# Products of zeros on TensorE between the steps of a selective-scan kernel

## The chip, the cores and the metric

The kernel runs on one core of a Trainium2 chip. The metric is the device time of one execution in microseconds (us), the median of several runs. The profile is of one further execution, taken by the hardware profiler.

## What is computed

The reference takes an image batch of 4 x 64 x 64 positions with 96 channels through four layers. Two are selective scans (state-space layers), two are attention without a softmax followed by a small quantized network. Nearly all the time goes into the two scan layers. Cut to what matters, one of them does this for each of 4 orders k in which the 4,096 positions are read:

```python
xc = silu(conv3x3_depthwise(in_proj(group_norm(x))) + conv_b)
dts, Bs, Cs = split(x_proj_k @ xs_k)            # 6 + 16 + 16 rows
delta = softplus(dt_w_k @ dts + dt_b_k)         # 192 channels
h_t = exp(delta_t * A) * h_(t-1) + (delta_t * u_t) * B_t     # 192 channels x 16 states
y_t = sum over the 16 states of h_t * C_t
y = sum over k of (y + Ds * xs), put back into image order
x = x + out_proj(layer_norm(y) * silu(z))
```

## The kernel before

**Tiles.** The scans are cut into 3,072 tiles. A tile is one state pair for 64 of the 192 channels over 1,024 positions: 128 partitions hold 64 channels of two images or states, the free dimension holds 1,024 positions. The list `tiles` (L1030) runs over 64 blocks `at`, each a phase (layer and pair of images), an order k and a quarter t of the positions; in a block over 2 groups g of 8 state numbers n, over 3 thirds j of the channels, and innermost over the 8 n of the group. So a block has 48 tiles, and a group of 8 tiles sums into one accumulator `py` in PSUM (tag psY, one buffer of two banks).

**What one tile needs.** For tile i, with `f` a buffer in SBUF (6 of them) and `psB` one in PSUM (2 of them):

- `begin` (L656): ScalarE writes the decays exp(delta*A) into f (`decays`, L679). For the five n in POOL_N (1, 4, 7, 10, 13) GpSimd writes the inputs du*B into f instead (L662), and ScalarE writes the decays into psB.
- `row` (L667): for the other eleven n, TensorE spreads the rows of B over the partitions with two bf16 products with the selection matrix `sel` into psB (L672). It has to wait until the scan of tile i-2 has left that psB.
- `product` (L683): VectorE multiplies psB by delta*u (L686).
- `scan` (L688): VectorE runs the recurrence over 1,024 positions into f (L694). ScalarE keeps the last column as the next state (L700).
- `weigh` (L702): GpSimd multiplies by C (L705).
- `gather` (L738): for every second tile, TensorE adds two tiles into `py` with four fp32 products with `fold`, a 128 x 64 matrix of two identities (L745). This frees both f.
- At the end of a group of 8, `flush` (L750) has ScalarE copy py away (L757 or L761), and `resume` (L725) has ScalarE write into the same py what the next group's sum begins with (L731, L733 or L736).

**The order.** The engines' orders of work are written out by hand (`manual_schedule`) in the loop at L1065. In step i the calls come in this order: `begin(i+2)`, `flush(i-3)` and `resume(i-2)` at a group's end, `gather(i-2)` where that n is odd, `row(i+2)`, `scan(i)`, the decays of a POOL_N tile i+2, `product(i+1)`, `weigh(i)`. Each engine works through its own instructions in that order. After these calls come side jobs: the next block's preparation (`prepare`, L511: projections L552, cuts L568 and L572, steps L579), and pieces of a generator (`behind`, L1015) that runs the next convolution (`conv_pieces`, L214) or the layer norm and output projection of an earlier phase (`tail_pieces`, L320). In the trace a full-precision (fp32) product appears as two records, a bf16 product as one.

After the last scan step come the two attention layers and their networks, under a planner (`run`, L776) that the change doesn't touch.

Of the kernel before, what the change touches and what calls it, by code (L numbers as in the profile page):

```python
# [8 lines left out]
F32 = mybir.dt.float32  # L9
# [18 lines left out]
NG = 2  # L28
GN = N // NG
MANUAL = {mybir.EngineType.PE, mybir.EngineType.DVE, mybir.EngineType.Activation, mybir.EngineType.Pool}  # L30
POOL_N = (1, 4, 7, 10, 13)


@with_exitstack
def kernel(ctx: ExitStack, tc: tile.TileContext, ins, out, layers=(0, 1, 2, 3)):
# [72 lines left out]

    minus = wp.tile([96, 2 * N], BF16, tag="minus", name="minus")
    nc.vector.tensor_scalar_mul(minus, m32[0:96], -1.0)  # L110


    def per_channel(name, cols, src, tag):
# [100 lines left out]
    def conv_pieces(w, xin, xc, zg, done):  # L214

        norms = []

        def part_of(n):
            xb = wide([C, T], "xb")
            nc.sync.dma_start(xb, xin[n // NT][:, n % NT * T : (n % NT + 1) * T])  # L220
            return xb

        xbs = [part_of(n) for n in range(3)]
        for _ in range(4):
            yield free()
        for i in range(2):
            stats = small([C, NT, 6], "gst")
            for t in range(NT):
                if t:
                    yield free()  # L230
                nc.vector.bn_stats(stats[:, t, :], xbs.pop(0))
                if i * NT + t + 3 < 2 * NT:
                    xbs.append(part_of(i * NT + t + 3))
            mv = small([C, 2], "gmv")
            nc.vector.bn_aggr(mv, stats)
            yield free(2)
            pm = psM([C, 1])
            nc.tensor.matmul(pm, gmat, mv[:, 0:1], start=True, stop=True)
            yield held(1)
            mean = small([C, 1], "gmean")  # L240
            nc.vector.tensor_copy(mean, pm)
            dev = small([C, 1], "gdev")
            nc.vector.tensor_sub(dev, mv[:, 0:1], mean)
            nc.vector.tensor_mul(dev, dev, dev)
            nc.vector.tensor_add(dev, dev, mv[:, 1:2])
            yield free(2)
            pv = psM([C, 1])
            nc.tensor.matmul(pv, gmat, dev, start=True, stop=True)
            yield held(1)
            t = small([C, 1], "grs")  # L250
            nc.vector.tensor_scalar_add(t, pv, 1e-5)
            scale = small([C, 1], f"gscale{i}")
            nc.gpsimd.tensor_tensor(scale, t, mhalf[0:C, 0:1], ALU.pow)
            yield free()
            shift = small([C, 1], f"gshift{i}")
            nc.vector.scalar_tensor_tensor(shift, mean, -1.0, scale, ALU.mult, ALU.mult)
            norms.append((scale, shift))
        if "join" in w:
            w.pop("join")()
        rows = T // HW  # L260

        def load(t):
            pads = []
            for i in range(2):
                r0, r1 = t * rows - 1, (t + 1) * rows + 1
                lo, hi = max(r0, 0), min(r1, HW)
                pad = wide([C, rows + 2, HW + 2], "pad")
                nc.vector.memset(pad[:, :, 0:1], 0.0)
                nc.vector.memset(pad[:, :, HW + 1 : HW + 2], 0.0)
                if lo > r0:  # L270
                    nc.vector.memset(pad[:, 0, 1 : HW + 1], 0.0)
                if hi < r1:
                    nc.vector.memset(pad[:, rows + 1, 1 : HW + 1], 0.0)
                inner = pad[:, lo - r0 : hi - r0, 1 : HW + 1]
                nc.sync.dma_start(inner, xin[i][:, lo * HW : hi * HW].rearrange("p (r c) -> p r c", c=HW))
                pads.append((pad, inner))
            return pads

        outs = []
        done.append(now[0])  # L280
        coming = load(0)
        yield free()
        yield free()
        for t in range(NT):
            pads, coming = coming, None
            for i in range(2):
                nc.scalar.activation(pads[i][1], pads[i][1], AF.Identity, bias=norms[i][1], scale=norms[i][0])  # L287
            yield free(6)
            for j in range(J):
                if outs:  # L290
                    outs.pop()()
                if j == J - 1 and t + 1 < NT:
                    coming = load(t + 1)
                px = psM([128, T])
                for tap in range(9):
                    for i in range(2):
                        nc.tensor.matmul(  # L297
                            px[64 * i : 64 * i + 64], w["wf"][:, tap, 64 * j : 64 * j + 64],
                            pads[i][0][:, tap // 3 : tap // 3 + rows, tap % 3 : tap % 3 + HW],
                            start=(tap == 0), stop=(tap == 8),  # L300
                        )
                    yield held(10 - tap, tap < 8)
                xo = thin([128, T], "xo")
                nc.scalar.activation(xo, px, AF.Silu, bias=w["cb"][:, j, :])
                pz = psM([128, T])
                for i in range(2):
                    nc.tensor.matmul(
                        pz[64 * i : 64 * i + 64], w["wz"][:, 64 * j : 64 * j + 64],
                        pads[i][0][:, 1 : 1 + rows, 1 : 1 + HW], start=True, stop=True,
                    )  # L310
                yield held(1)
                zo = thin([128, T], "zo")
                nc.scalar.activation(zo, pz, AF.Silu)
                nc.sync.dma_start(xc[:, j, t * T : (t + 1) * T], xo)
                outs.append(lambda j=j, t=t, zo=zo: nc.sync.dma_start(zg[:, j, t * T : (t + 1) * T], zo))
                yield free(6 if j < J - 1 else 0)
            outs.pop()()
            done[0] += 1

    def tail_pieces(w, units, y, zg, xin, xout, tokens):  # L320
# [11 lines left out]
        for t in units:  # L332
# [28 lines left out]
            for q in range(2):  # L361
                pt = psM([128, 2, D])
                for j in range(J):
                    nc.tensor.matmul(
                        pt[:, :, 64 * j : 64 * j + 64], yu[:, j, q * 128 : (q + 1) * 128], ident, start=True, stop=True
                    )
                if q:
# [58 lines left out]
            if tokens:  # L426
                xo = thin([128, 2, 2, C], "xn")
                pos = []
                for i in range(2):
                    half = slice(64 * i, 64 * i + 64)  # L430
                    pos.append(psM([128, 2, 128]))
                    for q in range(2):
                        tok = slice(q * 128, (q + 1) * 128)
                        o = pos[i][:, q, 0:C]
                        nc.tensor.matmul(o, xr[:, i, tok], ident[0:C, 0:C], start=True, stop=False)
                        for j in range(J):
                            nc.tensor.matmul(o, zu[half, j, tok], w["ow"][half, j, :], start=False, stop=(j == J - 1))  # L437
                    yield held(2 - i)
                for i in range(2):
                    nc.scalar.copy(xo[:, i], pos[i][:, :, 0:C])  # L440
# [5 lines left out]
            else:  # L446
                xo = thin([C, 2, U], "xn")
                pos = []
                for i in range(2):
                    half = slice(64 * i, 64 * i + 64)  # L450
                    pos.append(psM([C, U]))
                    nc.tensor.matmul(pos[i], ident[0:C, 0:C], xr[:, i, :], start=True, stop=False)
                    for j in range(J):
                        nc.tensor.matmul(pos[i], w["ow"][half, j, :], zu[half, j, :], start=False, stop=(j == J - 1))
                    yield held(2 - i)
                for i in range(2):
                    nc.scalar.copy(xo[:, i, :], pos[i])
# [53 lines left out]
    def prepare(ph, k, t):  # L511
# [37 lines left out]
        def project(s, j):  # L549
            if j == 0:  # L550
                pps.append(psM([76, T]))
            nc.tensor.matmul(  # L552
                pps[s], order[0][0][:, j, :], xs[j][:, halves[s]], start=(j == 0), stop=(j == J - 1)
            )

# [13 lines left out]

        def take(s, q):  # L570
            part = slice(32 * q, 32 * q + 32)
            nc.tensor.matmul(  # L572
                pps[s][0 : 2 * N], minus[part], p["parts"][part, halves[s]], start=False, stop=True,
                skip_group_check=True,
            )

        def steps(s, j):
            pds.append(psM([128, T]))
            nc.tensor.matmul(  # L579
                pds[-1], order[0][1][64:76, j, :], rests[s][64:76], start=True, stop=True  # L580
            )

# [84 lines left out]
    def row(i):  # L667
        at, g, j, n = tiles[i]
        if n not in POOL_N:
            for s in range(2):  # L670
                ss = slice(s * T, (s + 1) * T)
                nc.tensor.matmul(  # L672
                    scanned[i][0][:, ss], sel[:, n, :], made[at]["parts"][:, ss], start=True, stop=True
                )

# [36 lines left out]
    def unlock():  # L712
        py = psY()
        for s in range(2):
            for q in range(T // 128):
                o = s * T + q * 128
                nc.tensor.matmul(py[:, o : o + 128], ident, ident, start=(q == 0), stop=True, skip_group_check=True)

    def recall(i):
        at, g, j, n = tiles[i]  # L720
# [17 lines left out]
    def gather(i):  # L738
# [3 lines left out]
        for s in range(2):  # L742
            ss = slice(s * T, (s + 1) * T)
            for e in range(2):
                nc.tensor.matmul(  # L745
                    py[64 * e : 64 * e + 64, ss], fold, two[e][:, ss],
                    start=False, stop=(n == g * GN + GN - 1), skip_group_check=True,
                )

    def flush(i):  # L750

# [284 lines left out]
    with tc.manual_schedule(engines=MANUAL):  # L1036
# [28 lines left out]
        for i in range(-9, end + 4):  # L1065
# [9 lines left out]
                resume(i - 2)  # L1075
            if 0 <= i - 2 < end and tiles[i - 2][3] % 2:
                gather(i - 2)
            if 0 <= i + 2 < end:
                row(i + 2)
            if 0 <= i < end:  # L1080
# [151 lines left out]
```

## Time and profile before

| | |
|---|---|
| median of 3 runs | 11,288.7 us (11,288.23 to 11,288.97) |
| the profiled execution's own time | 11,291.6 us |
| its span | 11,289.8 us |
| granted TensorE clock, mean | 0.814 of full speed |
| scans, L694 | 3,072, mean 2.27 to 2.35 us by kind |
| weighings on GpSimd, L705 | 3,072 of 2.354 us |
| inputs on GpSimd, L662 | 960 of 2.359 us |
| gathers, L745 | 12,288 records of fp32 products |
| first scan | 130 us after the start |

DVE is VectorE, ACT is ScalarE, POOL is GpSimd, PE is TensorE and PEld its weight loads, which overlap its products. A busy share is over the whole span. In a row of groups the numbers after the bar are busy us and the mean ns of one instruction, and after a second bar the idle time of that engine just before them, and who ended most of it. A row of waits reads "who waited <- for whom: us in total, times, longest us". PEclk is the clock granted to TensorE, in tenths of full speed by slice; in finer windows it is either 1.00 or 0.50, and the record changes only at steps of 3.41 us.

### The profile page before, as it was taken

The page shows a single profiled execution, that of the slowest core. Times are in us where ns is not written, and L with a number is a line of the kernel's source. Part 1 is how long each engine was busy: PE and PEld are TensorE (multiplying, and loading weights), DVE is VectorE, ACT ScalarE, POOL GpSimd, SP SyncE. Part 2 cuts the span into 40 slices and gives each one's busy share as a digit, 9 for nine tenths or more (in the row PEclk, how much of TensorE's full clock was granted, in tenths as well). Part 3 has the DMA queues.
Part 4 walks back from the last instruction along what each step waited for, and adds up shares of the span by engine and source line. Part 5 has one row for each costly group of instructions (what it writes and reads, how often), then busy time and mean ns, then how long its engine had stood idle before and what let it go on. Part 6 is the DMA issues. An engine that isn't in the chain of part 4 may idle for free. (4 is left out here: it accounts for less than half of the span.)

```text
span 11289.8 us, 97780 instructions
## 1 busy us (share of the span) xinstructions
PE 8418.7 (75%) x27696; PEld 2658.3 (24%) x27696; DVE 9945.0 (88%) x6431; ACT 7094.3 (63%) x11231; POOL 10199.5 (90%) x5102
## 2 busy tenths in 40 slices
PE   7877778766777777877677776788777776677776
PEld 2212122111222221222122221222122222112365
DVE  3898899999999899988999999899999999999845
ACT  3657666555666665677566665676566665556676
POOL 3889899999999898989999999999999999999846
PEclk8878888877888787888878888888887877887876
DMA  5669876897678885698656656665566565556410
GB/s 131 154 141 156 137 154 155 153 132 133 150 165 147 135 163 150 139 157 146 145 146 170 155 143 149 156 166 141 149 159 158 140 157 145 141 135 155 123 39 18
DMA packets 1848972, 1605.07 MB, mean 142 GB/s; under 512 B 1412330, under 2 KB 1483692, under 8 KB 1848428
## 3 DMA queue, kind: packets, MB, share of 16 engines
q1 hardware_dynamic: 1848428, 1598.83, 65.0%
q8 instruction: 218, 3.57, 0.1%
q14 instruction: 326, 2.67, 0.1%
HBM read 1009.16 MB, written 186.65 MB: 106 GB/s over the span
## 5 line engine op out<-in xcount | busy, mean ns | idle before, releaser
L705 POOL TENSOR_TENSOR f<-f,crep 128x1024 f32<-128x1024 f32 x3072 | 7159.4, 2354 | 482.4 <-DVE f L694 354.0
L745 PE MATMUL psY<-f,fold 128*64 128x512 f32 x12288 | 4261.9, 771 | 675.3 <-issue 292.9
L694 DVE TENSOR_TENSOR_SCAN f<-f,state,psB 128x1024 f32<-128x1024 f32 x1584 | 3718.3, 2347 | 226.3 <-ACT f L679 65.7
L672 PE MATMUL psB<-spB,sel 96*128 96x512 bf16 x4224 | 1484.2, 439 | 1927.9 <-DVE f L694 1878.9
L686 DVE TENSOR_TENSOR psB<-psB,du 128x1024 f32<-128x1024 f32 x2112 | 2558.2, 1211 | 368.2 <-PE psB L672 327.2
L679 ACT ACTIVATE f<-delta,L_a 128x1024 f32<-128x1024 f32 x2112 | 2407.4, 1145 | 667.2 <-PE psY L745 571.5
L662 POOL TENSOR_TENSOR f<-du,brep 128x1024 f32<-128x1024 f32 x960 | 2264.2, 2359 | 211.9 <-DMA crep<-bc 81.0
L694 DVE TENSOR_TENSOR_SCAN f<-psB,state,f 128x1024 f32<-128x1024 f32 x720 | 1678.5, 2331 | 168.9 <-ACT psB L679 132.5
L745 PEld LDWEIGHTS psY<-f,fold 128*64 128x64 f32 x12288 | 1079.3, 166 | 3138.4 <-issue 2189.0
L700 ACT COPY state<-f 128x1 f32<-128x1 f32 x2304 | 427.2, 186 | 1842.0 <-DVE f L694 1832.7
L679 ACT ACTIVATE psB<-delta,L_a 128x1024 f32<-128x1024 f32 x960 | 1069.2, 1114 | 563.9 <-DVE f L694 536.6
L694 DVE TENSOR_TENSOR_SCAN f<-f,psB 128x1024 f32<-128x1024 f32 x528 | 1207.9, 2288 | 56.5 <-ACT f L679 6.3
L672 PEld LDWEIGHTS <-sel 96*128 96x128 bf16 x4224 | 284.1, 101 | 3768.8 <-DVE f L694 2436.4
L297 PE MATMUL psM<-pad,wf 96*64 96x512 f32 x3456 | 912.9, 645 | 11.6 <-ACT pad L287 8.4
L694 DVE TENSOR_TENSOR_SCAN f<-psB,f 128x1024 f32<-128x1024 f32 x240 | 545.6, 2273 | 98.5 <-ACT psB L679 57.3
L595 POOL TENSOR_TENSOR xs<-delta,xs 128x1024 f32<-128x1024 f32 x192 | 452.5, 2357 | 90.4 <-ACT delta L592 90.4
L579 PE MATMUL psM<-proj,dtw 12*128 12x512 f32 x768 | 526.4, 783 | 0.2 <-ACT spB L568 0.2
L552 PE MATMUL psM<-xs,xp 128*76 128x512 f32 x768 | 429.2, 671 | 12.7 <-DMA xp<-in_L_xp 5.1
L761 ACT COPY ynew<-psY 128x1024 f32<-128x1024 f32 (+2 forms) x312 | 242.6, 819 | 195.3 <-PE psY L745 195.0
L297 PEld LDWEIGHTS psM<-pad,wf 96*64 96x64 f32 x3456 | 234.2, 144 | 511.3 <-issue 463.2
L586 ACT ACTIVATE delta<-psM,L_dtb 128x512 f32<-128x512 f32 x384 | 261.3, 681 | 144.3 <-PE psM L579 143.7
L679 ACT ACT_TABLE_LOAD x229 | 293.8, 1283 | 7.3 <-DMA delta<-delta 2.7
(146 smaller groups left out, 6074.1 us busy)
## 6 DMA issues: line engine op xcount, KB each, us to landing
crep<-bc SPq DMA_DIRECT2D x2048, 256.0 KB
delta<-delta SPq DMA_DIRECT2D x768, 256.0 KB
du<-xs SPq DMA_DIRECT2D x768, 256.0 KB
brep<-bc SPq DMA_DIRECT2D x640, 256.0 KB
yd<-ynew SPq DMA_DIRECT2D x192, 512.0 KB
xraw<-xcd SPq DMA_DIRECT2D x144, 512.0 KB
yold<-yd SPq DMA_DIRECT2D x144, 512.0 KB
yu<-yd SPq DMA_DIRECT2D x65, 384.0 KB
```

The source lines that it names most:

```text
L297: nc.tensor.matmul(px[64 * i : 64 * i + 64], w["wf"][:, tap, 64 * j : 64 * j + 64], pads[i][0][:, tap // 3 : tap // 3 + rows, tap % 3 : ta ...
L552: nc.tensor.matmul(pps[s], order[0][0][:, j, :], xs[j][:, halves[s]], start=(j == 0), stop=(j == J - 1))
L579: nc.tensor.matmul(pds[-1], order[0][1][64:76, j, :], rests[s][64:76], start=True, stop=True)
L595: nc.gpsimd.tensor_mul(xs[j], deltas[j], xs[j])
L662: nc.gpsimd.tensor_mul(f[:, 1:], made[at]["dus"][j][n % 2], reps[at, 0, n])
L672: nc.tensor.matmul(scanned[i][0][:, ss], sel[:, n, :], made[at]["parts"][:, ss], start=True, stop=True)
L679: nc.scalar.activation(out, made[at]["deltas"][j][n % 2], AF.Exp, scale=W[phases[ph][0]]["a"][:, k, j, n // 2 : n // 2 + 1])
L686: nc.vector.tensor_mul(scanned[i][0], scanned[i][0], made[at]["dus"][j][n % 2])
L694: nc.vector.tensor_tensor_scan(f[:, 1:], a, bu, 0.0 if t == 0 else states[at - 1][:, c : c + 1], ALU.mult, ALU.add)
L700: nc.scalar.copy(states[at][:, c : c + 1], f[:, TB : TB + 1])
L705: nc.gpsimd.tensor_mul(f[:, 0:TB], f[:, 1:], reps[at, 1, n])
L745: nc.tensor.matmul(py[64 * e : 64 * e + 64, ss], fold, two[e][:, ss], start=False, stop=(n == g * GN + GN - 1), skip_group_check=True,)
```

## The change

A bf16 tile of zeros, 96 x 128, is made at the start. All products of the scan phase, but for one transpose, go through a helper `multiply`, which adds what each should take at full clock to a running sum `work` while the program is being built: columns / 2400 us, times 4 for fp32, half of it for outputs on up to 64 partitions. In each step, between `gather(i-2)` and `row(i+2)`, a new function `warm(i-2)` compares the sum with BUSY = 2.2 us. What was missing up to 2.2 us is filled with products of the zeros with 512 columns of `sel`, accumulated into the first bank of py, each counted at 0.213 us. What was too much is carried to the next step. At the last n of a group it issues nothing, and the missing part is carried on, up to 2.2 us in all. The number of products is fixed when the program is built.

```diff
+BUSY = 2.2
...
+    work = [0.0]
+    zeros = wp.tile([96, 128], BF16, tag="zeros", name="zeros")
+    nc.vector.memset(zeros, 0.0)
+
+    def multiply(out, lhsT, rhs, start, stop, **kw):
+        cols = 1
+        for n in out.shape[1:]:
+            cols *= n
+        work[0] += cols / 2400 * (4 if rhs.dtype == F32 else 1) * (0.5 if out.shape[0] <= 64 else 1.0)
+        nc.tensor.matmul(out, lhsT, rhs, start=start, stop=stop, **kw)
...
-                nc.tensor.matmul(
+                multiply(
                     scanned[i][0][:, ss], sel[:, n, :], made[at]["parts"][:, ss], start=True, stop=True
                 )
...
-                nc.tensor.matmul(
+                multiply(
                     py[64 * e : 64 * e + 64, ss], fold, two[e][:, ss],
                     start=False, stop=(n == g * GN + GN - 1), skip_group_check=True,
                 )
+
+    def warm(i):
+        at, g, j, n = tiles[i]
+        py = sums.get((at, g, j))
+        spare = min(BUSY - work[0], BUSY)
+        work[0] = -spare
+        if py is None or n % GN == GN - 1:
+            return
+        while work[0] <= -T / 2400:
+            multiply(py[:, 0:T], zeros, sel[:, 0:4, :], start=False, stop=False, skip_group_check=True)
...
                 gather(i - 2)
+            if 0 <= i - 2 < end:
+                warm(i - 2)
             if 0 <= i + 2 < end:
                 row(i + 2)
```

The other replaced calls are those of the convolution, the projections, the tail's transposes by identity and its output products, and the products that open psY at the start.

More of the change, by code (lines that the diff above doesn't have):

```diff
@@ L237, in conv_pieces @@
             pm = psM([C, 1])
-            nc.tensor.matmul(pm, gmat, mv[:, 0:1], start=True, stop=True)
+            multiply(pm, gmat, mv[:, 0:1], start=True, stop=True)
             yield held(1)
@@ L247, in conv_pieces @@
             pv = psM([C, 1])
-            nc.tensor.matmul(pv, gmat, dev, start=True, stop=True)
+            multiply(pv, gmat, dev, start=True, stop=True)
             yield held(1)
@@ L363, in tail_pieces @@
                 for j in range(J):
-                    nc.tensor.matmul(
+                    multiply(
                         pt[:, :, 64 * j : 64 * j + 64], yu[:, j, q * 128 : (q + 1) * 128], ident, start=True, stop=True
@@ L434, in tail_pieces @@
                         o = pos[i][:, q, 0:C]
-                        nc.tensor.matmul(o, xr[:, i, tok], ident[0:C, 0:C], start=True, stop=False)
+                        multiply(o, xr[:, i, tok], ident[0:C, 0:C], start=True, stop=False)
                         for j in range(J):
-                            nc.tensor.matmul(o, zu[half, j, tok], w["ow"][half, j, :], start=False, stop=(j == J - 1))
+                            multiply(o, zu[half, j, tok], w["ow"][half, j, :], start=False, stop=(j == J - 1))
                     yield held(2 - i)
@@ L451, in tail_pieces @@
                     pos.append(psM([C, U]))
-                    nc.tensor.matmul(pos[i], ident[0:C, 0:C], xr[:, i, :], start=True, stop=False)
+                    multiply(pos[i], ident[0:C, 0:C], xr[:, i, :], start=True, stop=False)
                     for j in range(J):
-                        nc.tensor.matmul(pos[i], w["ow"][half, j, :], zu[half, j, :], start=False, stop=(j == J - 1))
+                        multiply(pos[i], w["ow"][half, j, :], zu[half, j, :], start=False, stop=(j == J - 1))
                     yield held(2 - i)
@@ L551, in project @@
                 pps.append(psM([76, T]))
-            nc.tensor.matmul(
+            multiply(
                 pps[s], order[0][0][:, j, :], xs[j][:, halves[s]], start=(j == 0), stop=(j == J - 1)
@@ L571, in take @@
             part = slice(32 * q, 32 * q + 32)
-            nc.tensor.matmul(
+            multiply(
                 pps[s][0 : 2 * N], minus[part], p["parts"][part, halves[s]], start=False, stop=True,
@@ L578, in steps @@
             pds.append(psM([128, T]))
-            nc.tensor.matmul(
+            multiply(
                 pds[-1], order[0][1][64:76, j, :], rests[s][64:76], start=True, stop=True
@@ L671, in row @@
                 ss = slice(s * T, (s + 1) * T)
-                nc.tensor.matmul(
+                multiply(
                     scanned[i][0][:, ss], sel[:, n, :], made[at]["parts"][:, ss], start=True, stop=True
@@ L716, in unlock @@
                 o = s * T + q * 128
-                nc.tensor.matmul(py[:, o : o + 128], ident, ident, start=(q == 0), stop=True, skip_group_check=True)
+                multiply(py[:, o : o + 128], ident, ident, start=(q == 0), stop=True, skip_group_check=True)
     def recall(i):
@@ L744, in gather @@
             for e in range(2):
-                nc.tensor.matmul(
+                multiply(
                     py[64 * e : 64 * e + 64, ss], fold, two[e][:, ss],
```

## The prediction

> **What bounds the kernel now.** I read the page first: who is busy, what clock TensorE had, which groups cost most.
>
> ```profile
> PE 8418.7 (75%) x27696; PEld 2658.3 (24%) x27696; DVE 9945.0 (88%) x6431; ACT 7094.3 (63%) x11231; POOL 10199.5 (90%) x5102
> ...
> PEclk8878888877888787888878888888887877887876
> ...
> L672 PE MATMUL psB<-spB,sel 96*128 96x512 bf16 x4224 | 1484.2, 439 | 1927.9 <-DVE f L694 1878.9
> L686 DVE TENSOR_TENSOR psB<-psB,du 128x1024 f32<-128x1024 f32 x2112 | 2558.2, 1211 | 368.2 <-PE psB L672 327.2
> ```
>
> POOL and DVE are nearly full, TensorE (PE) is not. A change that gives PE more work can pay only through what DVE and POOL wait for. The waits say which those are (us in total, times, longest):
>
> ```profile
> PE psB L672 <- DVE f L694: 1878.9, 1010, 15.1
> ...
> POOL f L705 <- DVE f L694: 354.0, 237, 29.4
> DVE psB L686 <- PE psB L672: 327.2, 233, 6.5
> ```
>
> So PE mostly waits for the scan that frees its psB, and yet DVE waited 327.2 us for rows that PE brought late, and POOL waits for DVE. Why a row is late shows in the windows, cut at the 3.41 us steps in which the clock record changes (columns: PE, PEld, DVE, ACT, POOL busy and instructions, granted clock, DMA share, GB/s):
>
> ```profile
> 9935.08:9938.50 3.42, 2.76 (x11) 0.89 (x10) 3.31 (x3) 1.51 (x3) 3.42 (x3) 1.00 1.03 243
> 9938.50:9941.91 3.41, 0.08 (x1) 0.08 (x2) 3.31 (x3) 3.31 (x5) 3.41 (x2) 1.00 1.04 231
> 9941.91:9945.32 3.41, 3.41 (x6) 0.82 (x8) 3.31 (x3) 1.43 (x2) 3.41 (x3) 0.50 1.04 232
> 9945.32:9948.74 3.42, 3.42 (x9) 0.60 (x6) 2.27 (x1) 1.36 (x2) 1.90 (x2) 0.50 1.05 235
> 9948.74:9952.15 3.41, 3.41 (x12) 1.15 (x12) 2.87 (x2) 1.92 (x4) 3.41 (x2) 1.00 0.48 108
> ...
> 9972.63:9976.04 3.41, 1.42 (x6) 0.33 (x5) 3.31 (x3) 0.72 (x1) 3.41 (x3) 1.00 0.57 117
> 9976.04:9979.46 3.42, 2.86 (x6) 0.51 (x4) 3.31 (x3) 3.42 (x7) 3.42 (x2) 0.50 0.44 116
> ```
>
> After a window with little PE work the clock is 0.50, and in the timeline of the first case the row comes late:
>
> ```profile
> 9941.83 1.01 PE L672 MATMUL psB<-spB,sel 96*128 96x512 bf16 x2 [3.99 <-DVE f L694]
> ...
> 9944.77 3.68 PE L745 MATMUL psY<-f,fold 128*64 128x512 f32 x8
> ...
> 9948.39 0.75 PE L672 MATMUL psB<-spB,sel 96*128 96x512 bf16 x2
> ...
> 9949.18 1.23 DVE L686 TENSOR_TENSOR psB<-psB,du 128x1024 f32<-128x1024 f32 x1 [1.59 <-PE psB L672]
> ```
>
> The gather (L745) took 3.68 us, where at full clock it takes 1.89 to 2.0; the row queued behind it, DVE stood 1.59 us. Set beside the clock record, 279 of the 327 us that DVE waited for rows lie where the clock's mean over the 3 us before was below 0.7, only 10 where it was full. Two stretches of 48 tiles each, both with tail work beside them:
>
> ```profile
> 5969.00:6126.00 157.00, 118.22 (x357) 37.75 (x357) 150.75 (x87) 102.42 (x156) 156.10 (x71) 0.86 0.64 158
> 6448.00:6613.00 165.00, 127.31 (x354) 38.37 (x354) 150.68 (x86) 104.57 (x202) 154.33 (x70) 0.77 0.58 148
> ```
>
> The same work, 0.86 against 0.77, 157 against 165 us; in the second DVE waited 10.4 us for rows, in the first 1.5. POOL's 156.1 of 157 also shows the floor: no stretch gets much under 155.
>
> **The zeros and the clock.** One product of 512 bf16 columns streams in 0.2145 us (the second of a row's pair starts that long after the first). Counting the ledger along PE's order in the trace gives 6,800 zero products, 1,459 us. None falls into the first ten of the 64 blocks (48 tiles each) and few into blocks 25 to 30 and 41 to 46: the convolutions overdraw the 2.2 us. 42 blocks, 6,835 us with a clock of 0.80, are fed, mostly in steps of even i-2: up to 10 products, 2.1 us, between one row and the next, where PE waits for a scan.
>
> Is that enough? Of the trace's 3,306 windows I counted how often the clock fell after a full-clock window that streamed this share of it: under 0.2, 350 of 356; 0.2 to 0.3, 133 of 175; 0.3 to 0.4, 91 of 231; 0.4 to 0.6, 50 of 455; above, 10 of 858. At half clock it rises after 588 of 858 windows of over 0.3, after 45 of 372 below. [...] By the row, 2.2 us in a step of 3.3 to 3.5 is 0.63, well above the edge. I take the row. Bursts and windows' edges leave some falls: I expect a quarter of the cold in fed blocks to stay, 0.92 to 0.97 there, about 0.90 overall.
>
> **Gain.** In fed blocks DVE waited 244 us for rows, 213 of it cold. Three quarters saved: 160 us of DVE. How much reaches the end? Low bound: 57 of those 244 us show as a POOL gap at the same tile, 0.23, since POOL usually has a tile in hand (median 1.3 us between a scan's end and its weighing). High bound: across 36 of the fed blocks the time rises by 1.0 us per us of row wait (fit with POOL's DMA waits beside it). I take 0.75, nearer to the fit because a lag used up is missing at the next stall: 120 us. Bounds 37 and 213.
>
> **Cost of the zeros.** They are issued before row(i+2) and wait for nothing but py. At most places PE would have waited for the scan longer than they last; inserting each block into the trace ahead of its row, the rows outside tiles n=8 pass the start of their product by 17.5 us in all. Cover gone, each block delays the row by its 2.1 us.
>
> **The new wait.** At i-2 with n=0 or n=8, py was just rewritten by resume on ScalarE, itself behind flush and the last gather. The first zero product waits for that, and behind it on PE stand row(i+2), the side pieces and the next gather. With n=0 the row would be n=4, which has none. With n=8 it is n=12's: 89 groups of 192 get zeros there (9 on average). Resume ended (median) 1.05 us after that row had started, 2.3 us before its product; 10 zeros and the row's 0.6 need 2.75. Inserted: 56 of 89 products late, 115 us together. Taking off POOL's lag at the same tile leaves 58, and 7.5 of the 17.5. I take these 66 us; bounds 0 (lag covers all) and 132. The gather behind is 2 to 2.5 us later at these two places; the decays it releases have 18 us of overrun only, within the bounds. Instead of the row's late gathers, next in line is POOL itself and its DMA waits (crep 81 us).
>
> The memset of `zeros` on DVE is smaller than a product (1.21 us) and lies in the 130 us before the first scan: nothing. The wrapper is Python only. Zeros wait on no DMA, so no queue moves.
>
> **Sum.** Profiled execution 11,291.6 (span 11,289.8): -120 +66 = -54, 11,237. The median of the runs lies 2.9 lower: 11,235, 0.5% faster.
>
> **Rivals.** (a) Clock rises, time falls: 0.55, 11,235; own range 11,120 to 11,265. (b) Slower, by the hold at n=8: the clock rises, but POOL's lag hid the cold rows (0.23 of 160 = 37 us), while the late rows of n=12 hit DVE in full, 132: 11,384. For it: POOL at 156 of 157 in a warm stretch, and a dozen groups in which the row would be 5 to 6.5 us late. It decides once the hold's cost passes the saving. 0.25. (c) POOL's floor takes back what DVE gains and the hold eats the rest: 11,285, 0.15; for it, blocks 57 to 60 run in 154 to 157 us at a clock of 0.80. (d) Zero products do not keep the clock up: no saving, blocks at half clock twice as long, 132 or more lost: 11,425, 0.05. Against it: fold is zeros but for 2 in 128 of each column, and gathers hold the clock; their moving data are not zero, though.
>
> 0.2% (23 us) is about what a measurement here tells from no change. Faster 0.55, same 0.15, slower 0.30. The range, 11,110 to 11,380, leaves out the best of (a) and the worst of (b) and (d).
>
> **What would show it.** Right: some 6,800 new bf16 products under `multiply`'s line; clock about 0.90, unchanged before 1,900 us; DVE waiting for rows 327 down to about 150 to 230; a new wait of PE for ScalarE's psY at n=8; POOL's wait for DVE down. (b): DVE's wait for rows stays near 327 with a high clock, and sits at n=12. (d): clock 0.80. Wrong altogether would be slower scans or products, or a clock near 0.90 with DVE's row waits gone and the same time.

## The result

The changed kernel takes 11,603.7 us (median of 4 runs, 11,601.6 to 11,623.2), the kernel before beside it 11,288.8. The ratio is 1.028, 95% interval 1.0263 to 1.0298: 315 us slower, where 54 us faster was forecast. It lies 224 us above the upper end of the range.

From the page of the changed kernel, the lines that answer to those of before. All products now stand under `multiply`, line 125; the DVE product is L701, the scan L709, the weighing L720:

```profile
PE 9503.6 (82%) x34505; PEld 3216.0 (28%) x34505; DVE 9941.0 (86%) x6432; ACT 7102.5 (61%) x11231; POOL 10206.4 (88%) x5102
...
PEclk8878888898888888888889888888898888898877
...
L701 DVE TENSOR_TENSOR psB<-psB,du 128x1024 f32<-128x1024 f32 x2112 | 2559.4, 1212 | 748.8 <-PE psB L125 711.0
...
L125 PE MATMUL psY<-sel,zeros 96*128 96x512 bf16 x6809 | 1903.3, 425 | 547.4 <-ACT psY L746 368.7
L125 PE MATMUL psB<-spB,sel 96*128 96x512 bf16 x4224 | 1411.9, 419 | 983.2 <-DVE f L709 954.2
```

The zeros are there, 6,809 of them, and TensorE waits less for scans. POOL and DVE do the same work in the same busy time (10,206 and 9,941 us). But DVE's idle time before its products has doubled, and the zeros stood idle for 547 us before they could start. The waits say it in one view:

```profile
ACT f L694 <- PE psY L125: 880.6, 420, 9.9
DVE psB L701 <- PE psB L125: 711.0, 343, 9.4
POOL f L720 <- DVE f L709: 608.4, 350, 27.7
...
PE psY L125 <- ACT psY L746: 368.7, 137, 8.8
...
PE psY L125 <- ACT psY L751: 111.6, 48, 6.7
...
PE psY L125 <- ACT psY L748: 67.5, 34, 3.6
```

L746, L748 and L751 are the three forms of `resume`, L746 the one at n=8. The wait of PE for them is the new wait that the prediction named. DVE's wait for rows went from 327 to 711 us, POOL's wait for DVE from 354 to 608. Of the 711 us 618 lie in a low clock, counted as the prediction counted its 279 of 327: the cold waits more than doubled while the mean clock rose from 0.814 to 0.858. One such place in the timeline of the changed kernel, tile n=8 with the row of n=12 behind it:

```profile
5498.38 0.99 ACT L782 COPY ysum<-psY 128x1024 f32<-128x1024 f32 x1
5499.40 1.02 ACT L746 COPY psY<-ysum 128x1024 f32<-128x1024 f32 x1
...
5500.47 4.42 PE L125 MATMUL psY<-sel,zeros 96*128 96x512 bf16 x10 [2.05 <-ACT psY L746]
...
5500.91 2.35 DVE L709 TENSOR_TENSOR_SCAN f<-f,state,psB 128x1024 f32<-128x1024 f32 x1
...
5504.69 1.06 PE L125 MATMUL psB<-spB,sel 96*128 96x512 bf16 x2
...
5505.79 1.23 DVE L701 TENSOR_TENSOR psB<-psB,du 128x1024 f32<-128x1024 f32 x1 [2.53 <-PE psB L125]
```

Flush, then resume, then ten zeros; the row starts when they are through, and DVE, whose scan ended at 5,503.26, stands 2.53 us. The ten take 4.42 us, not 2.1: the granted clock is 0.50. The windows, cut at the 3.41 us steps of this trace's clock record, show when it fell:

```profile
5492.40:5495.82 3.42, 2.71 (x12) 0.61 (x10) 3.31 (x3) 1.89 (x3) 3.42 (x3) 1.00 1.04 237
5495.82:5499.23 3.41, 0.92 (x3) 0.30 (x4) 3.41 (x2) 3.36 (x4) 3.31 (x2) 1.00 0.39 87
5499.23:5502.64 3.41, 2.17 (x6) 0.77 (x6) 3.31 (x3) 1.73 (x3) 3.41 (x3) 0.50 0.00 0
```

In the middle one TensorE ran three products, which stream for 0.19 of it (3 times 0.2145 of 3.41 us): it stood for a scan until 5,497.50, and for ScalarE from 5,498.42. In the kernel before, by the prediction's count, the clock fell after 350 of 356 such windows (under 0.2). So the products that were meant to hold the clock up start, at 5,500.47, when it has just gone down, at 5,499.23. The wait for ScalarE is a part of the idle time behind this fall, not all of it.

Counted over the trace, 218 blocks of zeros (1,595 products) waited for a resume, 547 us in all, and then ran for 541 us; in 74% of them the mean clock was under 0.7. In 199 the clock was full when the wait began; in 96 of these it fell during the wait, in 56 more while the zeros ran. DVE's row waits, counted by the tile they belong to, are 285 us at n=12 (none before), 161 at n=14 (42 before) and 122 at n=5 (17 before).

### The profile page after: what moved, and what is told of

It reads as the page before. It is cut to its first block, busy times and chain, and to the rows that moved or that the text cites. A ratio compares the mean times of both kernels' runs of the same rounds, so it can differ in the third digit from the quotient of the medians.

```text
span 11599.8 us, 111181 instructions
## 1 busy us (share of the span) xinstructions
PE 9503.6 (82%) x34505; PEld 3216.0 (28%) x34505; DVE 9941.0 (86%) x6432; ACT 7102.5 (61%) x11231; POOL 10206.4 (88%) x5102
## 5 line engine op out<-in xcount | busy, mean ns | idle before, releaser
L720 POOL TENSOR_TENSOR f<-f,crep 128x1024 f32<-128x1024 f32 x3072 | 7170.1, 2357 | 865.3 <-DVE f L709 608.4
L125 PE MATMUL psY<-f,fold 128*64 128x512 f32 x12288 | 3740.1, 702 | 334.0 <-POOL f L720 165.2
L709 DVE TENSOR_TENSOR_SCAN f<-f,state,psB 128x1024 f32<-128x1024 f32 x1584 | 3717.8, 2347 | 191.9 <-ACT f L694 32.0
L701 DVE TENSOR_TENSOR psB<-psB,du 128x1024 f32<-128x1024 f32 x2112 | 2559.4, 1212 | 748.8 <-PE psB L125 711.0
L125 PE MATMUL psY<-sel,zeros 96*128 96x512 bf16 x6809 | 1903.3, 425 | 547.4 <-ACT psY L746 368.7
L125 PE MATMUL psB<-spB,sel 96*128 96x512 bf16 x4224 | 1411.9, 419 | 983.2 <-DVE f L709 954.2
L709 DVE TENSOR_TENSOR_SCAN f<-psB,state,f 128x1024 f32<-128x1024 f32 x720 | 1676.9, 2329 | 141.0 <-ACT psB L694 117.4
L125 PEld LDWEIGHTS psY<-f,fold 128*64 128x64 f32 x12288 | 970.8, 155 | 2502.3 <-issue 1882.6
L709 DVE TENSOR_TENSOR_SCAN f<-f,psB 128x1024 f32<-128x1024 f32 x528 | 1207.5, 2287 | 54.4 <-ACT f L694 3.9
L125 PEld LDWEIGHTS <-zeros 96*128 96x128 bf16 x6809 | 677.1, 105 | 1804.2 <-issue 1261.4
L125 PEld LDWEIGHTS <-sel 96*128 96x128 bf16 x4224 | 312.2, 102 | 2458.3 <-DVE f L709 1469.6
L709 DVE TENSOR_TENSOR_SCAN f<-psB,f 128x1024 f32<-128x1024 f32 x240 | 545.0, 2271 | 85.3 <-ACT psB L694 56.9
L125 PE MATMUL psM<-proj,dtw 12*128 12x512 f32 x768 | 555.4, 813 | 0.2 <-ACT spB L583 0.2
L125 PE MATMUL psM<-xs,xp 128*76 128x512 f32 x768 | 405.9, 639 | 10.4 <-DMA xp<-in_L_xp 3.9
```

Source lines behind the costliest of these rows:

```text
L125: nc.tensor.matmul(out, lhsT, rhs, start=start, stop=stop, **kw)
L701: nc.vector.tensor_mul(scanned[i][0], scanned[i][0], made[at]["dus"][j][n % 2])
L709: nc.vector.tensor_tensor_scan(f[:, 1:], a, bu, 0.0 if t == 0 else states[at - 1][:, c : c + 1], ALU.mult, ALU.add)
L720: nc.gpsimd.tensor_mul(f[:, 0:TB], f[:, 1:], reps[at, 1, n])
```

## The experiments

Theory H: the loss is the price of the zero products in the step of a group's first tile (n=0 and n=8), which wait for resume and hold what stands behind them. Rivals: Q, zeros anywhere ahead of a row delay it; and, later, L, the number of zeros at these places costs whatever they wait for. Zeros that are left out are still charged to the ledger, so the others stay where they were unless said. Zero products add nothing to any sum, so all kernels compute the same.

| kernel | zeros | clock | DVE's wait for rows, us | time, us | ratio to before (interval) |
|---|---|---|---|---|---|
| before | 0 | 0.814 | 327 | 11,289 | 1 |
| the change | 6,809 | 0.858 | 711 | 11,604 | 1.028 (1.0263 to 1.0298) |
| e1, none at the first tile | 5,214 | 0.864 | 275 | 11,239 | 0.9959 (0.9944 to 0.9973) |
| e2, after the row | 6,903 | 0.848 | 782 | 11,719 | 1.0373 (1.0357 to 1.0388) |
| e3, only at the first tile | 1,595 | 0.809 | 762 | 11,670 | 1.0332 (1.0313 to 1.035) |
| e4, one at the first tile | 5,432 | 0.862 | 416 | 11,362 | 1.0057 (1.004 to 1.0073) |
| e5, first tile's into psB | 6,809 | 0.886 | 365 | 11,326 | 1.0029 (1.0016 to 1.0041) |
| e6, as e1, BUSY 1.6 | 0 | 0.813 | 306 | 11,305 | 1.0012 (1.0004 to 1.002) |
| e7, as e5, BUSY 2.8 | 15,121 | 0.955 | 508 | 11,366 | 1.0067 (1.0054 to 1.008) |
| e8, as e1, none at n=10 | 4,449 | 0.858 | 285 | 11,251 | 0.9966 (0.9953 to 0.9978) |
| e9, as e1, BUSY 2.8 | 11,910 | 0.923 | 209 | 11,137 | 0.9867 (0.9851 to 0.9884) |
| e10, five at the first tile | 6,178 | 0.853 | 582 | 11,471 | 1.0158 (1.0138 to 1.0179) |
| e11, as e1, BUSY 3.4 | 18,258 | 0.950 | 804 | 11,786 | 1.0433 (1.0418 to 1.0447) |
| e12, the change, BUSY 2.8 | 15,121 | 0.897 | 1,256 | 12,066 | 1.0681 (1.0666 to 1.0697) |

Times are medians; the kernel before ran at 11,289 to 11,297 beside them. Clock and waits are of the profiled execution; e5's was the fastest of its twelve (11,292), so its waits are at the low edge.

**e1: leave out the blocks that wait.**

```diff
         while work[0] <= -T / 2400:
+            if n % GN == 0:
+                work[0] += T / 2400
+                continue
             multiply(py[:, 0:T], zeros, ...)
```

> Zero products left out in the step of a group's first tile (n=0 and n=8), where py was just rewritten by ScalarE; they are still charged to the ledger, so all others stay as they were. Theory H (the loss comes from the blocks that wait for resume and then run at half clock): the new wait of TensorE for ScalarE's psY is gone, DVE waits for rows 150 to 300 us instead of 711, time 11,200 to 11,300. Rival Q (zeros anywhere ahead of a row delay it): DVE's row waits stay above 500, time 11,450 to 11,550.

Its waits:

```profile
PE psB L125 <- DVE f L709: 1170.4, 801, 15.0
...
ACT f L694 <- PE psY L125: 528.5, 327, 9.7
...
POOL f L720 <- DVE f L709: 377.0, 247, 29.4
...
DVE psB L701 <- PE psB L125: 274.5, 193, 4.8
```

As H has it, and not as Q: 5,214 zeros ahead of rows are left, and the loss is gone. The 1,595 products at a group's first tile cost 365 us of 11,604; the other 5,214 make the kernel 0.4% faster. The mean clock does not show the loss: it is about the same in both (0.864 and 0.858).

**e3: only those blocks.** The condition is `n % GN` instead of `n % GN == 0`.

> Zero products only in the step of a group's first tile, the others charged but not issued: some 1,450 instead of 6,809. H: all of the loss or more, since the clock is lower elsewhere: 11,560 to 11,680, clock at most 0.82. Q: the loss in proportion to the zeros, 1,450 of 6,809, 11,350 to 11,380.

H again: 375 us slower with 1,595 products, the same 365 within what the runs scatter. Counted over the trace, 77% of its blocks ran at a mean clock under 0.7. The median of one such product in the trace's tile view:

```profile
L125 PE MATMUL psY<-sel,zeros x1595: 376/631/634, 1940.3 to 11008.6; 96*128 96x512 bf16 x200
```

Over all zeros of the change that median is 379 ns: of the 5,214 outside its waiting blocks 98% started at a granted clock of 1.00, of the 1,595 in them 27%.

**e2: the row first.** The calls `warm(i - 2)` and `row(i + 2)` change places.

> The same zero products, but issued after row(i+2) instead of before it. H: the row of n=12 no longer stands behind the hold, but the next gather and the rows of n=5 and n=14 still do: about half of the loss stays, 11,380 to 11,480. Q: rows have nothing but real work ahead of them, the loss goes: 11,200 to 11,300.

Both expectations were too low, and Q's, that the loss goes, has the wrong sign. The ledger is now asked after the row, so there are 94 more zeros. With the row ahead, n=12 waits for nothing of the new, and the kernel is slower than the change. ScalarE's wait for gathers before:

```profile
ACT f L679 <- PE psY L745: 571.5, 360, 9.8
```

And in e2:

```profile
ACT f L694 <- PE psY L125: 1188.6, 501, 9.8
DVE psB L701 <- PE psB L125: 782.3, 414, 7.9
```

ScalarE waits 1,189 us for gathers (881 in the change), but its late decays do not hold the scans: the scans waited 225 us for them (264 before). DVE loses its time at the rows, by tile 175 us at n=14, 155 at n=3, 143 at n=5 and 108 at n=9 (42, 84, 17 and 81 before). Issued before the row, zeros mostly lie in the time in which TensorE waits for the scan anyway; issued after it, they start when the scan has ended and stand ahead of the next gather and the next row. That this order is the whole cause is argued, not tested.

**e4 and e10: shorter blocks behind the same wait.** One product, and at most five, at a group's first tile; the rest is charged but not issued.

```diff
+        left = 5
         while work[0] <= -T / 2400:
+            if n % GN == 0 and not left:
+                work[0] += T / 2400
+                continue
+            left = max(left - 1, 0)
             multiply(...)
```

> In the step of a group's first tile one zero product instead of up to ten, so that the wait for resume stays and the block's length goes. If the wait alone holds the rows: 11,450 or more, within 150 us of the change. If the block's own length, about 4 us at half clock behind the wait, is what passes the slack of 2.3 us: 11,250 to 11,350. Q: between, about 11,500.

> As the change, but at most five zero products in the step of a group's first tile: at half clock they last as long (2.1 us) as the ten of the change would at full clock, which is how they were priced. With one product it was 11,362, with up to ten 11,604. If the half clock's doubling is what made the block overrun its slack: 11,400 to 11,470, so at least half of the 242 us goes. If each product costs the same: about 11,490.

The waits of e4:

```profile
DVE psB L701 <- PE psB L125: 416.1, 250, 5.6
...
PE psY L125 <- ACT psY L746: 371.1, 137, 8.8
...
PE psY L125 <- ACT psY L751: 112.5, 48, 6.7
...
PE psY L125 <- ACT psY L748: 67.1, 34, 3.1
```

The wait for ScalarE is whole (551 us) and costs, with its one product, 123 us (11,362 less e1's 11,239): 0.56 us for each of 218 blocks. Products two to five add 109 us, the rest 133: 0.15 and then 0.21 us a product. So at most a third of the loss is the wait, and two thirds are length. In e4 the wait alone was to give 11,450 or more and the length alone at most 11,350; it is between. Nor does the half clock alone decide whether a block overruns its slack: e10 lies at the upper edge of what that would give, and near the 11,490 of an equal price for each product. Its blocks last 1.36 us on average (counted), a little less than the 1.57 us that the change's would take at full clock (7.3 products of 0.2145), and still cost 232 us.

**e5 and e7: zeros that wait for no resume.** At a group's first tile the sum goes into the psB of the next tile; in e7 BUSY is 2.8 as well.

```diff
+        if n % GN == 0:
+            py = scanned[i + 3][0]
         while work[0] <= -T / 2400:
```

> All 6,809 zero products in their places, but in the step of a group's first tile they are added into the psB of the next tile (n=3 or n=11), which its row has just filled and its product reads only after the running scan, instead of into py. So nothing of them waits for resume. Theory H (wait for resume, and the half clock that it brings): the wait for ScalarE is gone, no block runs long at half clock, DVE's row waits 200 to 280 us, time at or a little under the kernel with those blocks left out: 11,190 to 11,250. Rival L (it is the number of zeros at these places that costs, whatever they wait for): 11,450 or more.

> As with the other bank, and BUSY 2.8. If more zeros only hold the clock better: clock 0.93, 11,150 to 11,220. If TensorE then has too little left to catch up behind late gathers: slower than with 2.2, 11,260 to 11,400, with DVE's row waits above 300 us in the warm clock.

e5's row waits:

```profile
DVE psB L701 <- PE psB L125: 365.0, 285, 4.6
```

The resume wait is gone and with it 278 us of the loss. L, which had 11,450 or more, does not explain it. In 190 of the 218 blocks the clock stays full from the first zero to the last, in the change in 47; over the 42 fed blocks of 48 tiles it is 0.91. But e5 is 87 us above e1 where H alone expected none: a product waits for the zeros in its own psB. By tile, 156 us of DVE's waits are now at n=11 and 80 at n=3, the two that got the zeros (24 and 47 in e1). In e7, within the second expectation, those two tiles have 425 of 508 us, which hides what 2.8 does.

**e6, e9, e11: how much to fill, without the first tile's blocks.**

> Zero products left out at a group's first tile, and BUSY 1.6 instead of 2.2. H, with the gain in proportion to the clock that is kept up: clock about 0.84, half of the 50 us saved with 2.2: 11,250 to 11,280. If the zeros' queueing eats part of the saving: under 11,240.

e6 tells nothing on that: it has no zero product at all. Real products come to about 1.72 us a step (5,297 us by the ledger's rates over 3,072 steps; at a clock of 1.00 the trace of before is close to these rates: 0.43 us for a gather's product, which the ledger has at 0.427, and mostly 0.215 or 0.226 for a row's, at 0.213), so a ledger of 1.6 is never short. Its 1.0012 shows what a kernel with the work of before may differ by.

> No zero products at a group's first tile, BUSY 2.8 instead of 2.2. If the saving follows the clock (1.6: 0.81 and nothing saved, 2.2: 0.86 and 50 us): clock 0.92, 11,150 to 11,220. If more zeros take back by queueing what the clock gives: 11,240 to 11,350 with more of DVE's row waits in the warm clock.

> No zero products at a group's first tile, BUSY 3.4: about a whole step of 3.3 us. If the saving goes on with the clock: 0.95 or more, 11,050 to 11,130. If TensorE has now no room to catch up after a late gather: above the 11,137 of 2.8, 11,150 to 11,300, with DVE's row waits above 209 us and in the warm clock.

e9, with 2.8, beats e1 and the kernel before: 1.3% faster than before, and 13 us under the expected range. Of its row waits 83 us are cold by the prediction's count (279 before). Its page and waits:

```profile
PE 9848.9 (88%) x39606; PEld 3580.6 (32%) x39606; DVE 9936.6 (89%) x6432; ACT 7105.2 (64%) x11231; POOL 10207.0 (92%) x5102
...
PEclk7889999999999999999999999999999999999977
```

```profile
POOL f L720 <- DVE f L709: 346.1, 208, 27.7
DVE psB L701 <- PE psB L125: 208.9, 163, 6.2
```

Blocks 8 to 11 take 152 to 154 us each (153 to 158 before): near the floor that POOL sets, which was busy for 152 to 153 us of each of them in the kernel before. e11, with 3.4, about the length of a step, is some 490 us above the higher of its two ranges:

```profile
PE 10848.0 (92%) x45954; PEld 4074.1 (35%) x45954; DVE 10028.6 (85%) x6432; ACT 7131.6 (61%) x11231; POOL 10227.9 (87%) x5102
```

```profile
DVE psB L701 <- PE psB L125: 803.8, 821, 6.3
...
PE psB L125 <- DVE f L709: 154.3, 112, 15.1
```

The clock is 0.95, and of DVE's 804 us of row waits about 600 lie in full clock. TensorE is simply behind: it waits only 154 us for scans (489 in e9).

**e8: also none at n=10**, where zeros stand straight behind a gather.

> As the kernel without zero products at a group's first tile, and without them at n=10 too, where they stand straight behind a gather and ahead of the row of n=14 (DVE waited 83 us for that row there, 42 in the kernel before). If that queueing is what is left of the cost: n=14 back to about 42 us, clock a little lower, 11,190 to 11,240. If the lower clock costs as much: 11,240 to 11,280.

The wait at n=14 fell to 39 us from 83, as expected, but the others rose from 192 to 246: 11,251, which can't be told from e1's 11,239.

**e12: the change with 2.8.**

> The change itself with BUSY 2.8, zero products at a group's first tile included. If the price of these is a sum of its own beside the saving (365 us at 2.2, between 11,239 and 11,604): 11,480 to 11,560. If a better kept clock makes the waiting blocks cheap: under 11,350.

Neither. With 3,211 zeros at the first tiles instead of 1,595, these cost 930 us (12,066 less e9's 11,137), more per product (0.29 us) than at 2.2 (0.23). The waits:

```profile
DVE psB L701 <- PE psB L125: 1256.1, 540, 10.7
...
PE psY L125 <- ACT psY L746: 513.3, 183, 8.8
PE psY L125 <- ACT psY L751: 286.5, 127, 7.0
```

There are also more such blocks, 354 instead of 218, and longer ones, 9.1 products instead of 7.3. That a fuller queue has less left to win back a delay would fit; no run separates it.

## Why the prediction was wrong

**Right.** What bounds the kernel and what the currency is: DVE's wait for rows. In the table time follows it: 315 us for 384 more in the change, 424 for 455 in e2, -152 for -118 in e9. That is about 0.8 to 1.3 where the difference is over 100 us, with e7 (77 for 180) and e10 (183 for 255) lower. The 6,800 zeros (6,809). The place of the new wait, n=8 with n=12 behind it. That the clock fell after windows with some work in them and not only after idle ones: in the kernel before, over 500 of its 634 falls came after windows that streamed 0.05 or more, and e9, with the clock at 0.923, has 118 us less of row waits and 152 us less time. That the clock is higher with zero products: 0.923 with 11,910 of them (e9), 0.813 in e6, which has none.

**Wrong, the step that failed: "I take these 66 us; bounds 0 (lag covers all) and 132."** The hold, 58 of these 66 us, cost 365 (e1), over six times that and nearly three times the upper bound. Four things in that term:

- *Too few blocks were counted.* The sum has 89 groups with zeros at n=8; the trace has 137, the 137 waits at L746 above. The number of all zeros was right, so it is their places that were not; why is open. In proportion 115 us would become 177, an estimate from 137 over 89; n=12 waited 285.
- *Only the next row was looked at.* With n=0 "the row would be n=4, which has none", and nothing was charged. But 81 of the 218 blocks stand there, and the delay goes on down TensorE's queue: beside e1, which has all the other zeros, the rows of n=5 gained 101 us of waits and those of n=14 78. With blocks of about the priced length (e10) the price was already 232.
- *The length was priced at 0.2145 us a product.* At full clock the zeros start 0.216 us apart (a row's pair, from which the price was read, mostly 0.226), at half clock 0.427. The blocks stand behind a wait in which the clock fell in 96 of the 199 that began it at full clock; they took 541 us where the priced length gives 342 (1,595 times 0.2145). The last 631 products, which make up the difference between e10 and the change, cost 133 us.
- *POOL's lag was taken off in full, halving 115 to 58.* For the gain the prediction took 0.75 us of time per us of row wait. The same exchange must hold for a loss: 315 us for 384 is 0.82. That a lag hides a stall once and is then used up is how the prediction itself argued for the gain.

How the wait, the falling clock and the queue behind share the 365 us can't be separated further: they come together in these blocks.

**Too large: the gain, 120 us less 7.5.** Without the hold it was 56 us (e1; interval 30 to 63). The exchange was not the fault: row waits in the 42 fed blocks fell by 60 us, not 160. I expected the clock there at 0.92 to 0.97; it was 0.88 in e1. 2.2 us in a step of 3.4 is 0.65 on average, but it comes in bursts in the even steps, as the prediction said; that this is why the clock fell short is not tested. With 2.8 (e9) it was 0.94 there, and these blocks took 115 us less than before: about the gain forecast for 2.2. The rest of e9's 152 lies mostly in blocks that get zeros only at 2.8. The delay of other rows was too low at 17.5 us: n=14 alone went from 42 to 83 us in e1.

**The rivals.** (b) was the right mechanism with the right sign and too small a price, 11,384; (d) is refuted by the clock in e9, (c) by the times of e1 and e9. The sentence on the range does not fit (a): its own range, 11,120 to 11,265, lies inside 11,110 to 11,380.

## What to carry over

Work issued to fill an idle engine was not free here where it waited and urgent work stood behind it in that engine's queue: 1,595 such products cost 365 us, while the kernel with the other 5,214 alone gained 50. Look at the filler's operands for a producer on another engine, and follow the delay past the next instruction, to everything until the queue has room again. Price a gain and a loss in the same stall at the same exchange rate. How much filler is best is found by trying: here, all without the blocks that waited, 1.6 issues none, 2.2 gains 0.4%, 2.8 gains 1.3% and 3.4 loses 4.3%.

## What was not expected of the hardware

With 15,121 products whose stationary operand is all zeros (e7) the granted clock was 0.98 in the 42 fed blocks, 0.80 before. And it was mostly low after the waits: of 110 blocks of the change that had waited over 2 us for ScalarE, 88% ran at a mean clock under 0.7. In e5, where the same 218 blocks wait for no resume, it is about a tenth.
